# Group norm averages in 64x64 tiles, a split norm and a Strassen projection for the first image, two more output buffers

## The chip, the cores and the metric

The kernel runs on one core of a Trainium2 chip. The metric is the time of one execution on the device in microseconds (us). The core's engines are TensorE (PE; PEld is its weight load), VectorE (DVE), ScalarE (ACT), GpSimd (POOL) and SyncE (SP), which here only issues DMAs.

## What is computed

Input x has 8 images of 512 channels and 32x32 positions, all float32. The result is x plus the following, cut to what matters:

```
t  = silu(bn(conv1x1(group_norm(x))))           # 512 -> 512; halves y0, y1 of 256 channels
ys = [y0, y1]
for i in range(2):                               # two bottlenecks
    yi = ys[-1]
    z  = silu(bn(conv3x3(yi)))                   # 256 -> 256
    q, k, v = conv1x1(z), 3 x 256 channels       # 4 heads of 64
    z  = softmax(q (k + r)^T / 8) v              # over 1024 positions
    z  = silu(bn(conv1x1(z)))
    ys.append(yi + z)
out = x + silu(bn(conv1x1(concat(ys))))          # 1024 -> 512
```

The group norm has 32 groups of 16 channels: it needs the mean and the variance over 16 neighbouring partitions and all positions.

## The kernel before

An image lies in four tiles of 128 channels by 1024 positions (`xs`). The loop over the images works on one image at a time; the norm and first convolution (`cv1`) of the next image are worked into the first attention of the present one. Only the first image has its norm and `cv1` ahead of everything.

**The norm.** `gn_stats` takes mean and variance of each channel (L472, L473 on DVE). `gn_mean` averages over the 16 channels of a group by one matmul with the 128x128 matrix `gmat` (L478), four columns wide, and four small DVE steps form the deviations (L481 to L484). `gn_rstd` averages these by a second matmul (L489), DVE adds epsilon (L491), POOL takes the power -0.5 (L492), and DVE applies the norm in place, one 128x1024 pass for each tile (L506). `group_norm` is a generator that yields between these steps; for a later image each step is called from `behind`, between groups of attention.

**The opening.** SP loads four x tiles, the first raw 3x3 weights, then `w1` (1 MB, weights of `cv1`). DVE does the norm, then computes the 3x3 weights of the fast convolution (`make_u`, L316 to L331) and the batch norm scales `sh` and `bh`, and then the transformed image (`tiles_in`, L406 to L429). `cv1` is 32 matmuls of 128x512; float32 matmuls are two records each in the profile. Its lines show as L372, those of the 3x3 convolution as L921, with VectorE's `columns_out` and `rows_out` (L437 to L465) behind them; `z` then passes ScalarE's SiLU (L355).

**The projection.** `project` makes q, k and v by plain products (L372, L556). `project_strassen` makes them by Strassen's scheme, seven products in place of eight (L585, L589), from weight sums `sq` that `make_sq` computes and stores in DRAM and `load_sq` brings back. It is used for both bottlenecks from the second image on. It adds some DVE steps, in part behind the first logits (`add_r`, L606 and L607, and `later`).

**The attention.** `attention_fast` has four groups of eight steps in pairs: logits (L692), exponentials on ACT into `pt` (L696, three buffers), sums of these on DVE (L710, L712), products with v (L726) into the single buffer of `ps_av`. At a group's end, DVE evicts them (L734) and PE adds the sums up over partitions (`s_ps`, L744). Other work is called in the dictionary `behind`, by group, and by pair where a key has two numbers. In the first image's second attention these are

```python
behind = {1: ahead, NG: first, NG + 1: second}
if b == 0:
    behind |= {-1: load_ahead, 0: prepare, 2: lambda: make_sq(0), 3: lambda: make_sq(1)}
```

`prepare` is `make_ws`: four 128x1024 DVE steps (L172 to L175). `ahead` there runs `make_sw` (L249 to L252).

**The order.** A scheduler puts each engine's instructions in a fixed order, earlier written ones first where they are ready in its own estimate. `tc.issue_after(ins)` puts those instructions of its block that run on the engine of `ins` behind `ins`; it isn't a wait. Large weights share `ring`, five buffers of 1 MB; a load waits for a free one, and the loads behind it in SP's queue with it. PSUM has three buffers `ps_big` and one `ps_av`.

**The end.** `cv2` of the last image writes eight pieces of 128x512: an addition (L1180), SiLU, the addition of x (L1183), and a store from one of two buffers with tag `t`. Pieces of x come by POOL's queue into two buffers, each load behind the store of an earlier piece.

Of the kernel before, what the change touches and what calls it, by code (L numbers as in the profile page):

```python
# [44 lines left out]
F32 = mybir.dt.float32  # L45
# [16 lines left out]
def kernel(  # L62
# [41 lines left out]
        nc.sync.dma_start(xt, src)  # L104
        return xt

    xs = [load_x(act, 0, c, NX) for c in range(NX)]


    def ring(shape, name):  # L110
# [2 lines left out]
    def load_w1():  # L113
        w = ring([P, NX, 2 * C], "w1")
        nc.sync.dma_start(w, cv1_w.rearrange("(k p) o -> p k o", p=P))
        return w

    def load_w2(n=2):
        nk = (2 + N) * NM // 2
# [56 lines left out]
        last = [nc.gpsimd.dma_start(dst, w) for w, dst in zip(sums, s_dram2)][-1]  # L176
        return last, (a11, s1, a12, s4, s2, s3, a22)

    w1 = load_w1()

    NBN = 2 * NM + 2 * N * NM + NO
    bnp = const.tile([P, NBN, 4], F32, name="bnp")
# [33 lines left out]

    sq_dram = [tc.dram_tile([P, 4, 3, P], F32, name=f"sq{n}") for n in range(N)]

    def make_sq(n):
        (a11, a12), (a21, a22) = ([block_qkv(n, o, i) for i in range(2)] for o in range(2))  # L220
        parts = [act.tile([P, 2, 3, P], F32, tag="x", name="sq_new", bufs=NX) for _ in range(2)]
# [128 lines left out]
    def stages(act, small, ps_big, ps_av, n_pt):  # L350
# [3 lines left out]

            return nc.scalar.activation(dst, src, AF.Silu, scale=sh[:, k : k + 1], bias=bh[:, k : k + 1])  # L355

        silu_in = []

        def table_of(func):

# [2 lines left out]
        def conv1x1(w_of, rhs_of, nk, ks=None, ps=None, ends=None, by_half=False):  # L363


            if ps is None:
                ps = ps_big.tile([P, NH, HALF], F32, tag="big", name="ps")
            begin, end = ends or (0, nk - 1)
            ks = range(nk) if ks is None else ks
            order = [(k, half) for k in ks for half in range(NH)]  # L370
            for k, half in sorted(order, key=lambda a: a[1]) if by_half else order:
                nc.tensor.matmul(ps[:, half, :], w_of(k), rhs_of(k, half), start=(k == begin), stop=(k == end))  # L372
            return ps

        def tiles_in(yp):
# [96 lines left out]
                nc.vector.bn_stats(st[:, half, :], xt[:, ts(half, HALF)])  # L472
            nc.vector.bn_aggr(mv[:, c, :], st.rearrange("p a b -> p (a b)"))  # L473

        def gn_mean(mv):

            ps = ps_big.tile([P, NX], F32, tag="big", name="gm_ps")
            nc.tensor.matmul(ps, gmat, mv[:, :, 0], start=True, stop=True)  # L478
            gm = small.tile([P, NX], F32, tag="gm", name="gm")
            dev = small.tile([P, NX], F32, tag="dev", name="dev")  # L480
# [6 lines left out]
        def gn_rstd(dev):  # L487
            ps = ps_big.tile([P, NX], F32, tag="big", name="gv_ps")
            nc.tensor.matmul(ps, gmat, dev, start=True, stop=True)  # L489
            gr = small.tile([P, NX], F32, tag="gr", name="gr")  # L490
            nc.vector.tensor_scalar(gr, ps, GN_EPS, None, ALU.add)  # L491
            nc.gpsimd.tensor_tensor(gr, gr, mhalf[:, :NX], ALU.pow)  # L492
            return gr

        def group_norm(xts, between=None):


            mv = small.tile([P, NX, 2], F32, tag="mv", name="mv", bufs=2)

            def stats(cs):  # L500
                for c in cs:
                    gn_stats(mv, c, xts[c])

            def apply(cs, gm, gr):
                for c in cs:
                    last = nc.vector.tensor_scalar(  # L506
                        xts[c], xts[c], gm[:, c : c + 1], gr[:, c : c + 1], ALU.subtract, ALU.mult
                    )
# [8 lines left out]
            gr = gn_rstd(dev)  # L517
            if between is None:
                yield apply(range(NX), gm, gr)
                return  # L520
            with tc.issue_after(between().ins):
                last = apply(range(NX), gm, gr)
            yield last

        def project(n, z):

# [372 lines left out]
        def cv1(w, xts, y0, y1, ocs):  # L899

            for oc in ocs:
                ps = conv1x1(lambda k: w[:, k, ts(oc, P)], lambda k, half: xts[k][:, ts(half, HALF)], NX)
# [250 lines left out]
        def cv2(b, w2, ys, begun={}, parts={}):  # L1153

            def rows_of(dram, oc, half):
                if isinstance(b, int):
                    return dram[b, ts(oc, P), ts(half, HALF)]
                return dram[bass.ds(b, 1), ts(oc, P), ts(half, HALF)][0]  # L1160

            def residual(oc, half):
                t = act.tile([P, HALF], F32, tag="xr", name="x_res", bufs=2)
                nc.gpsimd.dma_start(t, rows_of(x, oc, half))
                return t

            pieces = [(oc, half) for oc in range(NO) for half in range(NH)]
            res = [residual(*pieces[0]), residual(*pieces[1])]
            for i, (oc, half) in enumerate(pieces):
                if half == 0:  # L1170
                    ks = range((2 + N) * NM)
                    if oc in begun:
                        ps = cv2_products(w2, ys, oc, ks[-NM:], begun[oc], by_half=oc == NO - 1)
                    else:
                        ks = ks[2 * NM if oc in parts else 0 :]
                        ps = cv2_products(w2, ys, oc, ks, ends=(ks[0], ks[-1]), by_half=oc == NO - 1)
                t = act.tile([P, HALF], F32, tag="t", name="t", bufs=2)
                src = ps[:, half, :]
# [47 lines left out]
    with tc.issue_after(made.ins):  # L1226
# [6 lines left out]
    with tc.issue_after(last.ins):  # L1233
# [6 lines left out]
    s.cv1(w1, xs, y0, ypad[0], [*Y1S, *Y0S])  # L1240
    with tc.issue_after(made.ins):
        vs = s.tiles_in(ypad[0])
    load_bottleneck(0)
# [1 line left out]
    for b in range(B):  # L1245
# [6 lines left out]
        def u_of(n):  # L1252
            def of(oc):
                nonlocal last_load
                if b == 0 and oc == 1:
                    if n == 0:
                        with tc.issue_after(last.ins):
                            for i in range(PAIRS):
                                make(n, oc, [i])
                    else:  # L1260
                        for k in range(NM):
                            raws[n, oc, k] = load_raw(n, oc, k, "kv"[k])
                        with tc.issue_after(last.ins):
# [240 lines left out]
```

## Time and profile before

| | before |
|---|---|
| median of 3 runs | 2328.49 us (2327.59 to 2328.65) |
| the profiled execution | 2328.05 us |
| its span, first to last instruction | 2326.2 us |
| mean granted TensorE clock | 0.998 |
| PE busy | 2293.7 us |
| DVE busy | 1827.8 us |
| first product of `cv1` | 15.93 us |
| first 3x3 product | 46.20 us |

A row of the timeline has the start in us, the duration, engine, line, operation, the tiles as out<-in with shapes, and the number of records merged in it; a bracket has the idle time of the engine before it and what ended that. A row of the waits has who waited for whom, the total in us, how many times, and the longest. In the page's group lines the last number after the bar is idle time.

### The profile page before, as it was taken

The page shows a single profiled execution, that of the slowest core. Times are in us where ns is not written, and L with a number is a line of the kernel's source. Part 1 is how long each engine was busy: PE and PEld are TensorE (multiplying, and loading weights), DVE is VectorE, ACT ScalarE, POOL GpSimd, SP SyncE. Part 2 cuts the span into 40 slices and gives each one's busy share as a digit, 9 for nine tenths or more (in the row PEclk, how much of TensorE's full clock was granted, in tenths as well). Part 3 has the DMA queues.
Part 4 walks back from the last instruction along what each step waited for, and adds up shares of the span by engine and source line. Part 5 has one row for each costly group of instructions (what it writes and reads, how often), then busy time and mean ns, then how long its engine had stood idle before and what let it go on. Part 6 is the DMA issues. An engine that isn't in the chain of part 4 may idle for free.

```text
span 2326.2 us, 36363 instructions
## 1 busy us (share of the span) xinstructions
PE 2293.7 (99%) x14746; PEld 1160.4 (50%) x14746; DVE 1827.8 (79%) x2899; ACT 980.6 (42%) x1282; POOL 88.9 (4%) x307
## 2 busy tenths in 40 slices
PE   7999999999999999999999999999999999999998
PEld 4536346363553636446364553635436364463633
DVE  8867877888788887888788887887877988777774
ACT  1442624536244352544525344253542535335352
POOL 1000100000000000000000000000000000000001
PEclk9999999999999999999999999999999999999999
DMA  7413334041430415213161221602116030250202
GB/s 256 155 54 109 111 102 189 16 150 33 143 143 15 150 34 190 101 39 122 52 225 48 73 88 51 249 29 98 62 47 249 29 133 29 80 205 16 87 11 70
DMA packets 95280, 234.80 MB, mean 101 GB/s; under 512 B 28032, under 2 KB 50496, under 8 KB 81664
## 3 DMA queue, kind: packets, MB, share of 16 engines
q1 hardware_dynamic: 83296, 182.05, 23.2%
q0 software_dynamic: 11808, 50.34, 5.7%
q8 instruction: 118, 1.93, 0.3%
q14 instruction: 58, 0.48, 0.1%
HBM read 197.75 MB, written 34.60 MB: 100 GB/s over the span
## 4 chain that ended last, share of the span: by engine, by line
PE 95%; DVE 3%; DMA 1%; ACT 0%; issue 0%; POOL 0%; SPq 0%; DVEq 0%; ACTq 0%
PE av_ps L726 19%; PE l_ps L692 19%; PE c_ps L921 14%; PE c L976 8%; PE p_ps L585 7%; PE x_ps L1088 6%; PE c_new L976 6%; PE m_ps L942 5%; PE ps L372 5%; PE pv_ps L589 3%; PE s_ps L744 1%; PE p_ps L589 1%; PE s_ps L762 1%; PE v_ps L556 1%; DVE acc L712 0%; DMA x_res<-in_x_dram 0%
## 5 line engine op out<-in xcount | busy, mean ns | idle before, releaser
L696 ACT ACTIVATE pt<-l_ps 128x1024 f32<-128x1024 f32 x512 | 494.9, 1023 | 408.4 <-PE l_ps L692 385.4
L712 DVE TENSOR_TENSOR acc<-acc,pt 128x1024 f32<-128x1024 f32 x384 | 469.5, 1223 | 65.4 <-ACT pt L696 40.3
L726 PE MATMUL av_ps<-pt,vT 64*64 64x512 f32 x4096 | 485.1, 591 | 1.1 <-DVE ao L734 1.1
L692 PE MATMUL l_ps<-q,kr 64*64 64x512 f32 x4096 | 484.1, 590 | 0.0
L921 PEld LDWEIGHTS c_ps<-v_in,u 128*128 128x128 f32 x2720 | 306.3, 192 | 7.9 <-issue 6.7
L921 PE MATMUL c_ps<-v_in,u 128*128 128x128 f32 x2720 | 306.9, 275 | 1.1 <-DVE v_in L429 1.1
L726 PEld LDWEIGHTS av_ps<-pt,vT 64*64 64x64 f32 x4096 | 152.0, 133 | 277.3 <-issue 230.7
L692 PEld LDWEIGHTS l_ps<-q,kr 64*64 64x64 f32 x4096 | 153.7, 133 | 269.7 <-issue 256.2
L436 ACT COPY m<-c_ps 128x256 f32<-128x256 f32 x96 | 35.5, 370 | 225.8 <-PE c_ps L921 220.8
L976 PE MATMUL c_new<-t_in,ws 128*128 128x512 f32 x288 | 124.6, 592 | 0.0
L942 PE MATMUL m_ps<-ao,m_sb 128*128 128x512 f32 x256 | 112.5, 592 | 0.0
L710 DVE TENSOR_TENSOR acc<-pt 128x1024 f32<-128x1024 f32 x64 | 78.1, 1220 | 27.3 <-ACT pt L696 27.3
L355 ACT ACTIVATE m_kept<-m_kept,bh,sh 128x512 f32<-128x512 f32 x42 | 31.9, 806 | 146.0 <-DVE m_kept L1060 86.3
L976 PEld LDWEIGHTS c_new<-t_in,ws 128*128 128x128 f32 x288 | 54.7, 190 | 68.9 <-issue 66.0
L355 ACT ACTIVATE t<-m_ps,bh,sh 128x512 f32<-128x512 f32 x64 | 48.0, 776 | 83.9 <-PE m_ps L942 82.5
L585 PE MATMUL p_ps<-t_z,sq 128*128 128x512 f32 x168 | 81.3, 593 | 0.0
L942 PEld LDWEIGHTS m_ps<-ao,m_sb 128*128 128x128 f32 x256 | 48.6, 190 | 61.2 <-issue 61.2
L950 DVE TENSOR_TENSOR ylast<-t,ypad 128x512 f32<-128x512 f32 x32 | 22.0, 692 | 63.2 <-ACT t L355 63.2
L355 ACT ACTIVATE z<-z,bh,sh 128x512 f32<-128x512 f32 x64 | 48.6, 806 | 50.9 <-DVE z L465 50.9
L429 DVE TENSOR_TENSOR v_in<-w_rows 128x512 f32<-128x512 f32 x96 | 65.9, 687 | 0.0
L976 PE MATMUL c<-ypad,ws 128*128 128x512 f32 x144 | 63.8, 592 | 0.0
L1088 PE MATMUL x_ps<-t_x,sw 128*128 128x512 f32 x144 | 62.8, 592 | 0.0
(252 smaller groups left out, 2952.1 us busy)
## 6 DMA issues: line engine op xcount, KB each, us to landing
u<-u SPq DMA_DIRECT2D x85, 1024.0 KB
x<-in_x_dram SPq DMA_DIRECT2D x32, 512.0 KB
x_res<-in_x_dram POOLq DMA_DIRECT2D x28, 512.0 KB, 6.8
out_dram<-m_kept POOLq DMA_DIRECT2D x28, 512.0 KB, 7.2
w<-in_cv_w_dram SPq DMA_DIRECT2D x13, 1024.0 KB
u<-u_new POOLq DMA_DIRECT2D x12, 1024.0 KB, 5.9
rs<-r_dram SPq DMA_DIRECT2D x96, 128.0 KB
ws<-s SPq DMA_DIRECT2D x24, 512.0 KB
```

Of the source, the lines that this page charges most:

```text
L355: return nc.scalar.activation(dst, src, AF.Silu, scale=sh[:, k : k + 1], bias=bh[:, k : k + 1])
L372: nc.tensor.matmul(ps[:, half, :], w_of(k), rhs_of(k, half), start=(k == begin), stop=(k == end))
L585: nc.tensor.matmul(ps[:, o, :], w[:, o, :], rhs, start=not onto, stop=True, skip_group_check=onto)
L589: nc.tensor.matmul(v[:, ts(j, P)], rhs[:, ts(j, P)], w[:, 2, :], start=j == 0 and not onto, stop=True, skip_group_check=True,)
L692: nc.tensor.matmul(ps[kh * HD : (kh + 1) * HD, hd, :], kr[r, c, o : o + HD], q[r, c, ts(half, HALF)], start=True, stop=True,)
L696: exp = nc.scalar.activation(pt[:, i], ps, AF.Exp, scale=SCALE)
L712: ins = nc.vector.tensor_tensor(accs[g], accs[g], pt[:, i], ALU.add)
L726: nc.tensor.matmul(avs[g][hd * HD : (hd + 1) * HD, kh, :], vT[r, j, o : o + HD], pt[r, i, hd, :], start=(j == 0), stop=(j == NJ - 1),)
L921: nc.tensor.matmul(ps[:, row, col, :], us[i][:, k, row, SLOT[col], :], vs[i][:, k, row, col, :], start=(k == 0), stop=(k == NM - 1),)
L942: nc.tensor.matmul(pss[oc][:, half, :], m2_sb[:, n, k, ts(oc, P)], ao[:, k, ts(half, HALF)], start=(k == 0), stop=(k == NM - 1),)
L976: nc.tensor.matmul(ps[:, o, :], w[:, k, ts(o, P)], rhs[part][:, c, :], start=(k == 0 and not onto), stop=(k == KB - 1), skip_group_check=onto,
L1088: nc.tensor.matmul(ps[:, o, :], w[:, c, ts(o, P)], rhs[c], start=(c == 0 and not onto), stop=(c == 1), skip_group_check=onto,)
```

## The change

The averages: each of the two matmuls of a norm becomes two matmuls with 64x64 blocks of `gmat`, one for each half of the partitions, for all images.

```diff
+        def over_groups(ps, src):
+            for h in range(2):
+                r = slice(h * HD, (h + 1) * HD)
+                ins = nc.tensor.matmul(ps[r], gmat[r, r], src[r], start=True, stop=True)
+            return ins
...
-        def gn_mean(mv):
-            ps = ps_big.tile([P, NX], F32, tag="big", name="gm_ps")
-            nc.tensor.matmul(ps, gmat, mv[:, :, 0], start=True, stop=True)
...
+        def gn_mean(mv, n=NX, pool=ps_big, tag="big"):
+            ps = pool.tile([P, n], F32, tag=tag, name="gm_ps")
+            over_groups(ps, mv[:, :, 0])
```

The first image's norm goes in two halves of two tiles. `w1` is loaded in halves, the first one ahead of x2 and x3. POOL computes a shift, and ScalarE applies the norm. Products of `cv1` with the first half of the channels are placed between the steps of the second half's norm.

```diff
-    xs = [load_x(act, 0, c, NX) for c in range(NX)]
+    xs = [load_x(act, 0, c, NX) for c in range(NX // 2)]
...
+    load_w1_half(0)
+    xs += [load_x(act, 0, c, NX) for c in range(NX // 2, NX)]
...
-    w1 = load_w1()
+    load_w1_half(1)
...
+        def group_norm_part(xts):
+            n = len(xts)
+            mv = small.tile([P, n, 2], F32, tag="mv", name="mv", bufs=2)
+            for c in range(n):
+                gn_stats(mv, c, xts[c])
+            yield
+            gm, dev = gn_mean(mv, n, ps_av, "av")
+            yield
+            gr, multiplied, read = gn_rstd(dev, n, ps_av, "av")
+            shift = small.tile([P, n], F32, tag="dev", name="shift")
+            nc.gpsimd.tensor_tensor(shift, gm, gr, ALU.mult)
+            nc.gpsimd.tensor_scalar(shift, shift, -1.0, None, ALU.mult)
+            for c in range(n):
+                applied = nc.scalar.activation(
+                    xts[c], xts[c], AF.Identity, scale=gr[:, c : c + 1], bias=shift[:, c : c + 1]
+                )
+            yield multiplied, read, applied
...
-    normed = [*s.group_norm(xs, lambda: make_u(2, u_first[2][:, 0], raws[0, 0, 0]))][-1]
+    Y_ORDER = [*Y1S, *Y0S]
+    _, _, (_, read, _) = s.group_norm_part(xs[: NX // 2])
+    norm = s.group_norm_part(xs[NX // 2 :])
+    with tc.issue_after(read.ins):
+        next(norm)
+    begun = {}
+    def begin(oc, ks):
+        begun[oc] = s.cv1_products(w1, xs, oc, ks, begun.get(oc))
+        return s.last_product[0]
+    first = begin(Y_ORDER[0], [0])
+    with tc.issue_after(first.ins):
+        next(norm)
+    begin(Y_ORDER[0], [1])
+    first = begin(Y_ORDER[1], [0])
+    with tc.issue_after(first.ins):
+        multiplied, normed, applied = next(norm)
+    with tc.issue_after(multiplied.ins):
+        begin(Y_ORDER[1], [1])
+        begin(Y_ORDER[2], range(NX // 2))
+    made = make_u(2, u_first[2][:, 0], raws[0, 0, 0])
     with tc.issue_after(normed.ins):
         made = make_u(0, u_first[0][:, 0], raws[0, 0, 0])
```

`last_product` is the last matmul that `conv1x1` issued. `cv1` gets `begun` and goes on from the third channel tile where a product is begun. The last two steps of the first 3x3 weights are also put behind `applied`.

The first image's second bottleneck projects by Strassen. Its `make_sq(1)` moves from the third group of that attention to the end of the first attention, into another buffer.

```diff
-                if b > 0 and oc == 1:
+                if (b > 0 or n > 0) and oc == 1:
                     sq[n], last_load = load_sq(n)
...
         def second():
+            if b == 0:
+                make_sq(1, "xr", 2)
...
-            behind |= {-1: load_ahead, 0: prepare, 2: lambda: make_sq(0), 3: lambda: make_sq(1)}
+            behind |= {-1: load_ahead, 0: prepare, 2: lambda: make_sq(0, "x", NX)}
```

The last two of the eight output pieces take their tile from tag `h`, which also has two buffers:

```diff
-                t = act.tile([P, HALF], F32, tag="t", name="t", bufs=2)
+                t = act.tile([P, HALF], F32, tag="t" if i + 2 < len(pieces) else "h", name="t", bufs=2)
```

More of the change, by code (lines that the diff above doesn't have):

```diff
@@ L116, in load_w1, with load_w1_half @@
         return w
+    w1 = ring([P, NX, 2 * C], "w1")
+    def load_w1_half(i):
+        ks = slice(i * NX // 2, (i + 1) * NX // 2)
+        nc.sync.dma_start(w1[:, ks], cv1_w.rearrange("(k p) o -> p k o", p=P)[:, ks])
+    load_w1_half(0)
+    xs += [load_x(act, 0, c, NX) for c in range(NX // 2, NX)]
     def load_w2(n=2):
@@ L217, with make_sq @@
     sq_dram = [tc.dram_tile([P, 4, 3, P], F32, name=f"sq{n}") for n in range(N)]
-    def make_sq(n):
+    def make_sq(n, tag, bufs):
         (a11, a12), (a21, a22) = ([block_qkv(n, o, i) for i in range(2)] for o in range(2))
-        parts = [act.tile([P, 2, 3, P], F32, tag="x", name="sq_new", bufs=NX) for _ in range(2)]
+        parts = [act.tile([P, 2, 3, P], F32, tag=tag, name="sq_new", bufs=bufs) for _ in range(2)]
         s1, s2, s3, s4 = (t[:, j] for t in parts for j in range(2))
@@ L355, in silu @@
             return nc.scalar.activation(dst, src, AF.Silu, scale=sh[:, k : k + 1], bias=bh[:, k : k + 1])
-        silu_in = []
+        silu_in, last_product = [], [None]
         def table_of(func):
@@ L371, in conv1x1 @@
             for k, half in sorted(order, key=lambda a: a[1]) if by_half else order:
-                nc.tensor.matmul(ps[:, half, :], w_of(k), rhs_of(k, half), start=(k == begin), stop=(k == end))
+                last_product[0] = nc.tensor.matmul(
+                    ps[:, half, :], w_of(k), rhs_of(k, half), start=(k == begin), stop=(k == end)
+                )
             return ps
@@ L473, in gn_stats @@
             nc.vector.bn_aggr(mv[:, c, :], st.rearrange("p a b -> p (a b)"))
-        def gn_mean(mv):
-            ps = ps_big.tile([P, NX], F32, tag="big", name="gm_ps")
-            nc.tensor.matmul(ps, gmat, mv[:, :, 0], start=True, stop=True)
-            gm = small.tile([P, NX], F32, tag="gm", name="gm")
-            dev = small.tile([P, NX], F32, tag="dev", name="dev")
+        def over_groups(ps, src):
[6 more added lines that the diff above has]
+            over_groups(ps, mv[:, :, 0])
+            gm = small.tile([P, n], F32, tag="gm", name="gm")
+            dev = small.tile([P, n], F32, tag="dev", name="dev")
             nc.vector.tensor_copy(gm, ps)
@@ L485, in gn_mean, with gn_rstd, group_norm @@
             return gm, dev
[L487 to L495, printed above, removed]
+        def gn_rstd(dev, n=NX, pool=ps_big, tag="big"):
+            ps = pool.tile([P, n], F32, tag=tag, name="gv_ps")
+            ins = over_groups(ps, dev)
+            gr = small.tile([P, n], F32, tag="gr", name="gr")
+            read = nc.vector.tensor_scalar(gr, ps, GN_EPS, None, ALU.add)
+            nc.gpsimd.tensor_tensor(gr, gr, mhalf[:, :n], ALU.pow)
+            return gr, ins, read
+        def group_norm_part(xts):
[13 more added lines that the diff above has]
+                    xts[c], xts[c], AF.Identity, scale=gr[:, c : c + 1], bias=shift[:, c : c + 1]
+                )
+            yield multiplied, read, applied
+        def group_norm(xts):
             mv = small.tile([P, NX, 2], F32, tag="mv", name="mv", bufs=2)
@@ L516, in group_norm @@
             yield
[L517 to L523, printed above, removed]
+            yield apply(range(NX), gm, gn_rstd(dev)[0])
         def project(n, z):
@@ L897, in attention_general, with cv1_products, cv1 @@
             return ao
-        def cv1(w, xts, y0, y1, ocs):
+        def cv1_products(w, xts, oc, ks=range(NX), ps=None):
+            return conv1x1(
+                lambda k: w[:, k, ts(oc, P)], lambda k, half: xts[k][:, ts(half, HALF)], NX, ks, ps, (0, NX - 1)
+            )
+        def cv1(w, xts, y0, y1, ocs, begun={}):
             for oc in ocs:
-                ps = conv1x1(lambda k: w[:, k, ts(oc, P)], lambda k, half: xts[k][:, ts(half, HALF)], NX)
+                ks = range(NX // 2 if oc in begun else 0, NX)
+                ps = cv1_products(w, xts, oc, ks, begun.get(oc))
                 for half in range(NH):
@@ L1232 @@
             last = nc.vector.tensor_scalar(sh[:, at : at + NM], sh[:, at : at + NM], -1 / 12, None, ALU.mult)
-    with tc.issue_after(last.ins):
+    with tc.issue_after(last.ins), tc.issue_after(applied.ins):
         for i in (1, 2):
@@ L1239 @@
     y0 = new_y0()
-    s.cv1(w1, xs, y0, ypad[0], [*Y1S, *Y0S])
+    s.cv1(w1, xs, y0, ypad[0], Y_ORDER, begun)
     with tc.issue_after(made.ins):
```

## The prediction

> **What bounds the kernel now.** I read the page first: busy time by engine, then the chain that ended last.
>
> ```profile
> PE 2293.7 (99%) x14746; PEld 1160.4 (50%) x14746; DVE 1827.8 (79%) x2899; ACT 980.6 (42%) x1282; POOL 88.9 (4%) x307
> PE 95%; DVE 3%; DMA 1%; ACT 0%; issue 0%; POOL 0%; SPq 0%; DVEq 0%; ACTq 0%
> ```
>
> TensorE is the bound: 32.5 us of the 2326.2 us span are not PE. PE work that goes is worth its full time, unless another engine then ends the same stage. So I went to the stages that the edits touch, first the waits of PE:
>
> ```profile
> PE gm_ps L478 <- DVE mv L473: 11.0, 1, 11.0
> PE ps L372 <- DVE x L506: 2.2, 1, 2.2
> PE ps L372 <- ACT z L355: 2.1, 2, 1.2
> PE c_ps L921 <- DVE u_new L326: 1.3, 1, 1.3
> PE c_ps L921 <- DVE u_new L330: 1.2, 1, 1.2
> ```
>
> All lie in the first image. PE's first product starts at 15.93 us, but at 62 to 65 us PE waits for VectorE's u tiles, and at 76.01 for z. The timeline of VectorE between says why:
>
> ```profile
> 15.07 2.98 DVE L506 TENSOR_SCALAR x<-x,gm,gr 128x1024 f32<-128x1024 f32 x4 [1.16 <-POOL gr L492]
> 17.96 0.55 DVE L321 TENSOR_TENSOR u_new<-raw 128x384 f32<-128x384 f32 x1
> ...
> 74.69 0.42 DVE L465 SCALAR_TENSOR_TENSOR z<-sd,r_ends 128x256 f32<-128x256 f32 x1
> ```
>
> From L321 to L465 VectorE waits only 0.9 us (L406 for the second SiLU) and 0.2 us (L437). **The opening is VectorE's up to 76 us**: what counts there is when L321 starts, not when PE starts.
>
> For the averages of the later norms, the timeline of PE around one:
>
> ```profile
> 140.43 1.95 PE L726 MATMUL av_ps<-pt,vT 64*64 64x512 f32 x16
> 142.31 0.39 PE L489 MATMUL gv_ps<-dev,gmat 128*128 128x4 f32 x2
> 142.63 1.95 PE L692 MATMUL l_ps<-q,kr 64*64 64x512 f32 x16
> ```
>
> Sixteen such matmuls take 1.72 us start to start elsewhere (129.45 to 131.17). Here it is 2.20, of which 0.05 belong to the sums before; the next batch loses 0.05. So a 0.25 us matmul pair costs PE 0.48 us.
>
> **What the Trainium skill says.** "TensorEngine Tiling (Array Packing)", Key Properties: changing the tiling mode drains TensorE. The trace agrees: the 0.48 us. The same page, Gotcha 1, says that different row tiles can't access one PSUM bank at the same time; the new pair writes two halves of one bank, and no run here shows that. "TensorE: Matmul & The Clock Gate", Part 1: an idle array runs at half rate until some 3.4 us of activity. In the trace cv1's first six records are 0.85 us apart, up to 21.2 us, then 0.43: 5.3 us of half rate. "ScalarE: Activation LUTs", Table sets: identity is in every set, so I charge no table load for the new Identity passes; no run here shows it yet.
>
> **The opening.** x0 and x1 go first; half of w1 (512 KB) comes before x2 and x3. Loads of 512 KB landed some 1.5 us apart, so x3 is ready near 10.9 instead of 9.4. Statistics of x0 and x1: done at 7.1 (4.30 + 2 x 1.4). First average: 0.74 us to the copy, as now (10.83 to 11.57), four small DVE steps 0.85, second average 0.7: read at 9.6. POOL: 0.1 + 0.7 for two columns (1.04 for four, 3.15 for sixteen) + two new small steps 0.5. Then ScalarE, about 1.0 us for a 128x1024 pass as in its Exp rows (1.02): x0 at 12.0. **PE starts at 12.0, 3.9 us earlier.** w1's half is there.
>
> The other half: statistics follow the first read on DVE (9.6 to 12.4, x3 landing included). Its first average stands on PE behind two products, four records at 0.85: 15.4. DVE has its variance at 16.9. The second average stands behind eight more records, some still at half rate: 20.3; **the read on DVE is at 20.9**. Everything that VectorE does next is put behind this read, where today it starts at 17.96. Moving four applications (2.98 us) to ScalarE doesn't make up for it, since DVE idles meanwhile, but for L317 to L319. So DVE is 3.0 us later; it then meets no wait for the SiLUs (1.1 us gone), and some of the 2.1 us of second-bottleneck u work between 66.9 and 74.5 may fall behind z. I take **+1.5 us at 76 us**. Ends: read at 14.7 if PE held nothing up, -2 with fills left; read at 22.5 with both averages behind all twelve records, +3.5. PE's own lead ends as a longer wait for u. SP issues one DMA more; raw lands about 1.5 us later, while DVE is idle. POOL's new steps end before its 16-column power is wanted.
>
> **Averages in 64x64 tiles.** Seven later norms, two averages each: 14 x 0.48 = 6.7 us now. In the new form nothing drains; left are four short matmuls and two exposed 64-column loads (133 ns each against 187 for 128, partly overlapped): I estimate 0.19 us. Gain 14 x 0.29 = **-4.1 us**. Ends: 0 if one bank serialises them as a drain does, -6.7 if they are free.
>
> **First image's second projection by Strassen.** Now, and for a Strassen projection with the start of the attention:
>
> ```profile
> 208.59 3.60 PE L372 MATMUL ps<-z,qkv_sb 128*128 128x512 f32 x8
> 231.63 0.66 PE L692 MATMUL l_ps<-q,kr 64*64 64x512 f32 x4
> 250.22 1.95 PE L726 MATMUL av_ps<-pt,vT 64*64 64x512 f32 x16 [0.63 <-DVE ao L734]
> 367.30 1.88 PE L585 MATMUL p_ps<-z,qkv_sb 128*128 128x512 f32 x4
> 391.21 1.22 DVE L710 TENSOR_TENSOR acc<-pt 128x1024 f32<-128x1024 f32 x1
> 397.41 5.21 DVE L712 TENSOR_TENSOR acc<-acc,pt 128x1024 f32<-128x1024 f32 x4
> 402.54 0.68 DVE L734 TENSOR_TENSOR ao<-av_ps,ao 128x512 f32<-128x512 f32 x1
> ```
>
> The plain one takes 208.59 to 231.63, 23.0 us. Strassen takes 367.30 to 385.75, 18.45 us; here z comes 2 us later (L465 is 5.2 us after the convolution, there 3.2), and t1 queues on DVE: some 1.1 + 0.8 us of wait. So 20.3: **-2.7 us**.
>
> Then VectorE. With Strassen its first sum starts 5.46 us after the first logits (385.75 to 391.21), here 3.13 (231.63 to 234.76); add_r of the second half adds 2.4. In the image with Strassen shown, the eviction L734 begins 16.8 us after the logits and is just in time. But the first image's group 0 also holds make_ws, L172 to L175, 238.56 to 243.23: 4.67 us that run right behind the second pair's sums. Behind them queue the later sums and L734; PE's s_ps and next av wait for those, ps_av being a single buffer. L734 would end at 17.47 + 4.67 = 22.1 us, PE's av begin at 22.2 after the logits, against 18.59 now: **+3.6 us**. In group 1 DVE needs 14.0 us of PE's 14.5, so the stall isn't repeated. Net **+0.9 us**. Ends: -3.3 if make_ws falls into a gap, +2.5 with one more us for evictions of p_ps on ScalarE.
>
> make_sq(1) moves into the end of the first attention: four DVE ops, 2.2 us, fit the 2.32 us before 155.01 where DVE waits for a DMA, and its two POOL writes go where POOL idles. load_sq takes one ring buffer, so the second w2 load starts at about 205 instead of 198, over 30 us before its use; SP has nothing urgent behind it. Zero.
>
> **The end.** The last piece's t now waits at 2318.12 for an earlier store (1.62 us). With its own buffer, that goes; next comes x_res, for which L1183 waits at 2320.03, behind unchanged POOL stores. So **-0.2** for a less crowded last store; ends 0 and -0.7.
>
> Sum: 1.5 - 4.1 + 0.9 - 0.2 = -1.9 us. Against the profiled execution: span 2326.2 to 2324.3 (its own time 2328.05, 1.85 outside the span). Its time is 0.4 under the median 2328.49, which becomes **2326.6**. About 0.2%, 4.7 us, is what a measurement of this kernel tells from no change.
>
> **Rivals.** *Covered*: make_ws or its queue doesn't hold L734 up (-3.6) and the opening's DVE delay is taken out by the u work that moves (-1.5): 2321.5. For it: no wait of PE lies after 330 us. Against: VectorE's unbroken rows. *The change doesn't do what it says*: the 64x64 pair costs as much as the 128x128 one, no -4.1: 2330.7. For it: the shared bank. Against: attention's own 64x64 matmuls flow at 0.43 us per four. *Slower*: the second half's averages hold VectorE. Place: the read of the second average; price: 1 us for each us. From 22.8 us the whole is slower than before; at 24.3, with PE at half rate through all twelve records, it is 2330.0, and slower by 0.2% from 27.5. For it: PE's in-order queue and its half rate. Against: 5.3 us of half rate would be over at 17.3.
>
> **How the numbers follow.** Forecast 0.49, covered 0.32, same-cost tiles 0.07, held read 0.12. Faster by over 0.2%: covered and 0.02 of the forecast's edge, 0.34. Slower by over 0.2%: 0.07, the far half of the held read. Same: 0.59. The range 2320 to 2331 reaches past covered and same-cost, leaving about 0.15 out.
>
> **What would show it.** PE's first product near 12; the second-half read near 20.9 and z's L465 near 76; records around each average 1.9 us apart, not 2.2; first logits of the second attention about 20.3 us after its convolution; L734 with some 4 us of PE wait there; last L1183 still on x_res. If L734 isn't waited for, or PE waits for u less than now, I am wrong towards faster.

## The result and the profile after

| | before | after |
|---|---|---|
| median of 4 runs each, side by side | 2328.04 us (2327.21 to 2328.65) | 2328.56 us (2327.69 to 2329.48) |
| ratio | | 1.0003, 95% interval 0.9985 to 1.0020 |
| the profiled execution, its span | 2328.05, 2326.2 us | 2328.13, 2326.7 us |
| mean granted TensorE clock | 0.998 | 0.995 |

No change that can be measured. The forecast was 2326.6 us with "no change" as the likeliest case. But the zero is made of terms of up to 6 us, and only some of them have the predicted size. The page first: busy time by engine, and the chain that ended last. Line numbers are those of the kernel that a row comes from. In the changed kernel L617 and L621 are products of the projection by Strassen, L724 the logits, L758 the products with v (`av_ps`), L744 the sums, L766 the eviction and L776 `s_ps`.

```profile
PE 2292.5 (99%) x14806; PEld 1175.1 (51%) x14806; DVE 1837.1 (79%) x2918; ACT 986.2 (42%) x1287; POOL 90.9 (4%) x312
PE 93%; DVE 4%; DMA 1%; ACT 0%; issue 0%; SPq 0%; POOL 0%; DVEq 0%; ACTq 0%
```

PE is busy for 1.2 us less, though an eighth of a projection's products and the draining averages are gone: something made other PE work longer. And DVE has 4% of the chain where it had 3%. The waits of PE say where (who waited for whom; us in total, times, longest):

```profile
...
PE c_ps L959 <- DVE u_new L331: 4.7, 1, 4.7
PE s_ps L776 <- DVE acc L744: 4.3, 1, 4.3
PE ps L381 <- ACT x L529: 2.9, 1, 2.9
PE p_ps L617 <- issue: 2.0, 1, 2.0
...
PE av_ps L758 <- DVE ao L766: 0.5, 1, 0.5
```

The u wait is where PE's lead of the opening ended, as foreseen, 4.7 us for 2.5 before. The s_ps wait is the group 0 stall. "issue" at L617 hides t1: its step on DVE (L644) runs from 212.90 to 213.58, and PE goes on at 213.67. To place all this I compared when stages start in the two traces:

| up to | before | after | difference | what this stage adds |
|---|---|---|---|---|
| first 3x3 product | 46.20 | 42.31 | -3.89 | |
| first logits, first attention | 92.56 | 93.59 | +1.03 | opening +1.03 |
| second bottleneck's first 3x3 product | 187.02 | 187.34 | +0.32 | one norm's averages -0.71 |
| first logits, second attention | 231.63 | 231.18 | -0.45 | projection -0.77 |
| second image's first 3x3 product | 345.87 | 351.76 | +5.89 | attention +6.34 |
| last 1x1 product behind attention | 2287.94 | 2289.52 | +1.58 | six norms -4.31 |
| end of the span | 2326.19 | 2326.65 | +0.46 | end -1.1 |

**Opening.** VectorE's timeline: the second half's read, the u work behind it, and the last step of z.

```profile
20.01 0.16 DVE L510 TENSOR_SCALAR gr<-gv_ps 128x2 f32<-128x2 f32 x1 [3.10 <-PE gv_ps L491]
20.08 0.55 DVE L330 TENSOR_TENSOR u_new<-raw 128x384 f32<-128x384 f32 x1
...
75.73 0.41 DVE L476 SCALAR_TENSOR_TENSOR z<-sd,r_ends 128x256 f32<-128x256 f32 x1
```

The read is at 20.01 (forecast 20.9), u starts at 20.08 where it started at 17.96, and the last step of z starts 1.04 us later than before (74.69). In each of the thirteen profiles of this document the first logits follow this step by 17.86 or 17.87 us: when VectorE is done with z decides the opening.

**Averages.** PE's timeline around one of them:

```profile
141.11 1.95 PE L758 MATMUL av_ps<-pt,vT 64*64 64x512 f32 x16
142.87 0.17 PE L491 MATMUL gv_ps<-dev,gmat 64*64 64x4 f32 x1
142.88 0.65 PE L724 MATMUL l_ps<-q,kr 64*64 64x512 f32 x2
142.89 0.23 PE L491 MATMUL gv_ps<-dev,gmat 64*64 64x4 f32 x3
142.96 1.93 PE L724 MATMUL l_ps<-q,kr 64*64 64x512 f32 x14
144.65 1.94 PE L758 MATMUL av_ps<-pt,vT 64*64 64x512 f32 x15
```

The small matmuls run in among the logits. From 141.11 to 144.65 there are 3.54 us for two batches of 1.72: the average costs PE 0.1 us, where it cost 0.48. The two halves of one PSUM bank, a risk in the prediction, serialise nothing that can be seen.

**Projection and attention.** PE's timeline, from the first product on z to the sums of group 0:

```profile
208.90 1.88 PE L617 MATMUL p_ps<-z,qkv_sb 128*128 128x512 f32 x4
...
213.67 3.38 PE L617 MATMUL p_ps<-t_z,sq 128*128 128x512 f32 x4 [2.00 <-issue]
...
231.18 3.66 PE L724 MATMUL l_ps<-q,kr 64*64 64x512 f32 x32
...
252.89 1.08 PE L776 MATMUL s_ps<-acc,ones 128*32 128x256 f32 x8 [4.31 <-DVE acc L744]
253.91 3.69 PE L758 MATMUL av_ps<-pt,vT 64*64 64x512 f32 x16
```

Look at the durations of equal work. Four p_ps records take 1.88 us at 208.90, and 3.38 behind the wait of 2.00; sixteen av_ps records take 1.90 us elsewhere, and 3.69 behind the wait of 4.31. The busy time by stretch has, behind the bounds and the length, the busy time and count of PE, PEld, DVE, ACT and POOL, and then the granted clock, the DMA share and GB/s:

```profile
58.10:62.00 3.90, 3.59 (x15) 3.33 (x16) 3.90 (x10) 2.09 (x4) 0.41 (x1) 0.50 0.00 0
214.10:217.50 3.40, 3.40 (x8) 1.66 (x7) 1.78 (x5) 2.48 (x3) 0.00 (x0) 0.51 0.00 0
251.60:255.00 3.40, 2.11 (x16) 0.72 (x20) 3.30 (x4) 0.90 (x2) 0.00 (x0) 0.50 0.47 193
255.00:258.40 3.40, 3.40 (x24) 0.96 (x20) 3.29 (x5) 0.00 (x0) 0.00 (x0) 0.50 0.03 2
```

**Behind each of the three longer waits in the middle of the kernel, TensorE ran at half rate for 3.4 or 6.8 us.** The profile of before has that only at the start and the end. This is what the prediction had left out.

**Group 0's stall.** VectorE's timeline in it:

```profile
243.20 1.22 DVE L181 TENSOR_TENSOR s<-w,w 128x1024 f32<-128x1024 f32 x1
...
246.60 1.22 DVE L744 TENSOR_TENSOR acc<-acc,pt 128x1024 f32<-128x1024 f32 x1
247.74 1.22 DVE L184 TENSOR_TENSOR s<-w,s 128x1024 f32<-128x1024 f32 x1
248.87 3.87 DVE L744 TENSOR_TENSOR acc<-acc,pt 128x1024 f32<-128x1024 f32 x3
252.66 0.69 DVE L766 TENSOR_TENSOR ao<-av_ps,ao 128x512 f32<-128x512 f32 x1
```

The four steps of `make_ws` (L181 to L184) stand ahead of the last sums, and these ahead of s_ps and the eviction L766, with no gap between them: the mechanism of the prediction, row by row.

**The end**, VectorE's last two rows of the pieces:

```profile
2318.91 0.69 DVE L1221 TENSOR_TENSOR t<-t,x_res 128x512 f32<-128x512 f32 x1 [0.23 <-ACT t L364]
2320.89 0.69 DVE L1221 TENSOR_TENSOR t<-t,x_res 128x512 f32<-128x512 f32 x1 [1.29 <-DMA x_res<-in_x_dram]
```

The wait for an earlier store is gone, and the last addition waits for x_res instead, as predicted.

### The profile page after: what moved, and what is told of

It is laid out like the page before. It is cut to its first block, busy times and chain, and to the rows that moved or that the text cites. A ratio compares the mean times of both kernels' runs of the same rounds, so it can differ in the third digit from the quotient of the medians.

```text
span 2326.7 us, 36527 instructions
## 1 busy us (share of the span) xinstructions
PE 2292.5 (99%) x14806; PEld 1175.1 (51%) x14806; DVE 1837.1 (79%) x2918; ACT 986.2 (42%) x1287; POOL 90.9 (4%) x312
## 3 DMA queue, kind: packets, MB, share of 16 engines
q8 instruction: 119, 1.95, 0.3%
## 4 chain that ended last, share of the span: by engine, by line
PE 93%; DVE 4%; DMA 1%; ACT 0%; issue 0%; SPq 0%; POOL 0%; DVEq 0%; ACTq 0%
PE av_ps L758 19%; PE l_ps L724 18%; PE c_ps L959 14%; PE c L1014 8%; PE p_ps L617 8%; PE x_ps L1126 6%; PE c_new L1014 6%; PE m_ps L980 5%; PE ps L381 3%; PE pv_ps L621 3%; PE s_ps L776 1%; PE p_ps L621 1%; PE s_ps L794 1%; DVE acc L744 1%; DMA w<-in_cv_w_dram 0%
## 5 line engine op out<-in xcount | busy, mean ns | idle before, releaser
L744 DVE TENSOR_TENSOR acc<-acc,pt 128x1024 f32<-128x1024 f32 x384 | 469.4, 1222 | 68.7 <-ACT pt L728 43.0
L758 PE MATMUL av_ps<-pt,vT 64*64 64x512 f32 x4096 | 488.2, 593 | 0.5 <-DVE ao L766 0.5
L724 PE MATMUL l_ps<-q,kr 64*64 64x512 f32 x4096 | 486.5, 591 | 0.0
L758 PEld LDWEIGHTS av_ps<-pt,vT 64*64 64x64 f32 x4096 | 159.4, 133 | 270.5 <-issue 226.1
L724 PEld LDWEIGHTS l_ps<-q,kr 64*64 64x64 f32 x4096 | 160.2, 133 | 264.4 <-issue 253.2
L742 DVE TENSOR_TENSOR acc<-pt 128x1024 f32<-128x1024 f32 x64 | 78.1, 1220 | 20.9 <-ACT pt L728 20.9
L617 PE MATMUL p_ps<-t_z,sq 128*128 128x512 f32 x180 | 88.5, 602 | 2.0 <-issue 2.0
L448 DVE TENSOR_TENSOR r_mid<-c_ps,m 128x256 f32<-128x256 f32 x64 | 27.0, 422 | 45.6 <-ACT m L447 45.6
```

The source lines that it names most:

```text
L617: nc.tensor.matmul(ps[:, o, :], w[:, o, :], rhs, start=not onto, stop=True, skip_group_check=onto)
L724: nc.tensor.matmul(ps[kh * HD : (kh + 1) * HD, hd, :], kr[r, c, o : o + HD], q[r, c, ts(half, HALF)], start=True, stop=True,)
L742: return nc.vector.tensor_tensor(accs[g], pt[:, 0], pt[:, 1], ALU.add)
L744: ins = nc.vector.tensor_tensor(accs[g], accs[g], pt[:, i], ALU.add)
L758: nc.tensor.matmul(avs[g][hd * HD : (hd + 1) * HD, kh, :], vT[r, j, o : o + HD], pt[r, i, hd, :], start=(j == 0), stop=(j == NJ - 1),)
```

## The experiments

My theory: the change's parts add up as in the table, and what the Strassen part loses beyond the prediction is the half rate behind waits. Its rivals: the wait lengths alone did it (no clock), the stall isn't `make_ws`, and the opening is bound by something other than VectorE. In the ratios that follow, each kernel is set against the kernel before, run on the same chip (2327.66, 2327.62 and 2327.33 us in the three sets).

### The averages alone

The kernel before, with only the averages changed:

```diff
-            nc.tensor.matmul(ps, gmat, mv[:, :, 0], start=True, stop=True)
+            over_groups(ps, mv[:, :, 0])
...
-            nc.tensor.matmul(ps, gmat, dev, start=True, stop=True)
+            over_groups(ps, dev)
```

> The kernel before with one edit: the averages of every norm in two 64x64 matmuls. If a mode change's drain was the cost: each later image's first attention is 0.71 to 0.72 us shorter, seven times, so 5.0 us in all, nothing else moves, median 2323.1 against 2328.0. The prediction's estimate was 4.1. If the gain seen in the changed kernel belongs to something else in it: nothing.

Measured: 2322.09 us, ratio 0.9976 (0.9967 to 0.9986). Each of the seven later norms takes 0.71 to 0.72 us out, 5.0 together, and nothing else moves in the middle of the kernel. Confirmed. In this profile the opening was 0.39 us later, with only its two averages edited, and the end 1.25 shorter, with nothing edited: those two stages vary by themselves.

### Without the Strassen projection

The changed kernel with the first image's plain projection:

```diff
-                if (b > 0 or n > 0) and oc == 1:
+                if b > 0 and oc == 1:
...
-            if b == 0:
-                make_sq(1, "xr", 2)
...
-            behind |= {-1: load_ahead, 0: prepare, 2: lambda: make_sq(0, "x", NX)}
+            behind |= {-1: load_ahead, 0: prepare, 2: lambda: make_sq(0, "x", NX), 3: lambda: make_sq(1, "x", NX)}
```

> The changed kernel with the first image's second bottleneck projected plainly again (its weight sums made in the third group as before). Theory, VectorE queue and clock: the two half-rate stretches at 214 and 252 us and the 4.3 us wait of s_ps go; from that bottleneck's 3x3 start to its m2 start 117.6 us as before instead of 123.2, so 5.6 us less, median 2322.9. Rival, that Strassen's saved product pays and the rest is lost elsewhere: 2 to 3 us more than the changed kernel, 2331.

Measured: 2322.90 us, ratio 0.9978 (0.9970 to 0.9987). From the second bottleneck's 3x3 product to the second image nothing is lost (both come 0.19 us later than before), where the whole change loses 5.6. **Strassen costs this version 5.6 us, not 0.9.** The half rate at 214 and 252 is gone with it; that at 57 stays.

### The old opening

The changed kernel, with the order of loads, the whole norm on VectorE and the u transforms of before:

```diff
-    xs = [load_x(act, 0, c, NX) for c in range(NX // 2)]
+    xs = [load_x(act, 0, c, NX) for c in range(NX)]
...
-    load_w1_half(1)
+    w1 = load_w1()
...
+    normed = [*s.group_norm(xs, lambda: make_u(2, u_first[2][:, 0], raws[0, 0, 0]))][-1]
```

> The changed kernel with the opening of before (one norm for all four tiles on VectorE, w1 in one load, no product of cv1 ahead). Theory, VectorE bounds the opening: first logits at 92.6 instead of 93.6, the wait of PE for u short again and no half-rate stretch at 57 us; 1.0 us less, median 2327.5. Rival, PE's earlier start pays: 2 to 4 us more than the changed kernel.

Measured: 2327.08 us, ratio 0.9996 (0.9987 to 1.0004). First logits at 93.47: only 0.1 us sooner than with the new opening, so my number was missed. In the opening its trace has a half-rate stretch that before's hasn't, from 64.8 to 68.2, behind two waits for u of 1.3 and 1.2 us that before has as well. And behind t1 the clock stayed up this time, with a wait as long as the changed kernel's. Its row of PE:

```profile
213.57 1.95 PE L619 MATMUL p_ps<-t_z,sq 128*128 128x512 f32 x4 [2.00 <-issue]
```

The same wait of 2.00 us, then 1.95 us for what took 3.38. So a wait of this length doesn't always cost the clock. The projection came to -2.43 here, near the predicted -2.7.

### PE kept busy in the two waits

The changed kernel with idle PE time filled. The added matmuls go into PSUM that the following product overwrites; their results are never read. `fill` is 4 in the first image's second bottleneck.

```diff
+            for _ in range(fill):
+                nc.tensor.matmul(ps_b[:, 0, 0:256], gmat, z[:, 0, 0:256], start=True, stop=True)
             product(ps_b, ps_v[:, 1], s1, t1)
...
+                for _ in range(9 if sq is not None and at == NM * NH and g == 0 else 0):
+                    nc.tensor.matmul(ps, gmat, q[:, 0, 0:NQ4], start=True, stop=True)
```

> The changed kernel with matmuls that nobody reads put into PE's two waits of the first image's second bottleneck: four of 128x256 ahead of the second Strassen product (1.7 us), nine ahead of the first s_ps (3.8 us). Theory, clock: the waits stay as long, but no half rate follows at 214 and 252 us: 1.7 and 2.8 us less, 4.5 in all, median 2324.1. Rival, the time is the waits' own length alone: no change, or slower by what the fill overruns.

Measured: 2324.56 us, ratio 0.9986 (0.9979 to 0.9993). The busy time by stretch of this kernel:

```profile
214.10:217.50 3.40, 3.40 (x14) 2.09 (x15) 1.78 (x4) 2.06 (x3) 0.00 (x0) 1.00 0.00 0
251.60:255.00 3.40, 3.40 (x36) 1.20 (x40) 3.19 (x4) 0.38 (x2) 0.00 (x0) 1.00 0.12 45
```

And its timeline of PE, at the batch that took 3.69 us in the changed kernel:

```profile
252.12 1.95 PE L761 MATMUL av_ps<-pt,vT 64*64 64x512 f32 x16
```

The clock is 1.00 in both places, and the same av_ps batch is back at 1.95 us. Projection -2.46 (changed kernel -0.77), attention +3.63 (+6.34): 4.4 us gained by adding work, without shortening either wait (s_ps still starts 21.6 us behind the first logits, 21.7 in the changed kernel). **This separates the two parts of the loss: the wait, and the clock behind it.** Without the clock's part both terms are close to those of the prediction (-2.7 and +3.6), and av starts 22.2 us behind the first logits (252.12 less 229.90), the very number that was forecast.

### make_ws two groups later

```diff
+        def strassen_ready():
+            nonlocal three
+            prepare()
+            three = s.strassen(b, ws, y0, y1)
+            for i in range(PAIRS):
+                us[0, i] = load_u(0, 0, i)
...
-            behind |= {-1: load_ahead, 0: prepare, 2: lambda: make_sq(0, "x", NX)}
+            behind |= {-1: load_ahead, 2: strassen_ready, 3: lambda: make_sq(0, "x", NX)}
```

> The changed kernel, but make_ws of the first image (with the Strassen part that needs its sums) issued behind group 2 of the second attention, where it was behind group 0, and make_sq(0) behind group 3 instead of 2. If the long wait of PE in group 0 is make_ws standing between VectorE's sums and the eviction (my step of the prediction), the 4.3 us wait at the first sum matmul goes, and with it the half-rate stretch at 251.6: the stretch from first logits to the second image shrinks from 79.4 by about 6.3 us, to the 73.0 of the kernel before. Span 2320.5, time 2322. Part of it may come back in group 2: VectorE has about 0.5 us of slack a group there, so up to 2 us of wait. Rival: the wait comes from the Strassen projection's own evictions on VectorE, which begin the sums 2.3 us later; then at most 1 to 2 us go. Rival: DMA of the stores made by make_ws collides with the next image's loads in its new place; then waits of PE after 330 us appear.

Measured: 2323.78 us, ratio 0.9985 (0.9978 to 0.9992); span of the profile 2321.3. From the first logits of the second attention to the 1x1 product behind it 74.05 us pass, where the changed kernel has 79.4: 5.3 of the 6.3 us are gone, and s_ps isn't waited for. One wait of PE is new:

```profile
PE c L1014 <- DVE ao L766: 1.6, 1, 1.6
```

It is the backlog that was expected to come back in part. SyncE's rows, store and reload of the softmax reciprocals, show where VectorE lost time ahead of it:

```profile
273.73 0.32 SPq L822 DMA_DIRECT2D r_dram<-rc  x1
281.08 2.00 SPq L824 DMA_DIRECT2D rs<-r_dram  x2
```

They stand 7.4 us apart (1.6 and 1.4 in this kernel's groups before and behind), and VectorE waited 5.0 us for that. The long wait in group 0 was `make_ws`. What delays the reload is open. At that time POOL's queue had two stores of 1 MB by `make_ws`, issued at 270.16 and 271.42 and landed by 278.05, and behind them two loads of x_res, the last of which landed at 280.84. In the changed kernel a pair stands 4.5 us apart as well (262.76 and 267.23), but 13 us behind the stores of `make_ws`, which had landed by 253.78, and beside the loads of x_res. No run separates the two.

### t1 not held back

```diff
-            with tc.issue_after(mid.ins):
+            if first_image:
                 tt(t1, b12, b11, ALU.subtract)
+            else:
+                with tc.issue_after(mid.ins):
+                    tt(t1, b12, b11, ALU.subtract)
```

> The changed kernel, but in the first image t1, the first difference of the Strassen projection, isn't held behind the middle row's combination: VectorE can take it in the 2.7 us that it idles before 208.9. Then PE's second product starts right behind the first (211.7 instead of 213.67): no wait of 2.0 us and no half-rate stretch (1.7 us). A shorter wait, about 1.1 us, is left at the third product, for z of the second half. First logits of the second attention 2.8 us earlier (1.1 us counted), so second projection -3.6 against before where the changed kernel has -0.8; the wait in group 0 of 4.3 us and its half rate stay. Time 2325.7. If the half-rate stretch isn't a consequence of the wait it stays, and only 1.0 us is gained.

Measured: 2325.05 us, ratio 0.9991 (0.9984 to 0.9998). PE's timeline:

```profile
212.03 1.88 PE L617 MATMUL p_ps<-t_z,sq 128*128 128x512 f32 x4
...
216.21 1.98 PE L617 MATMUL p_ps<-z,qkv_sb 128*128 128x512 f32 x4 [1.41 <-ACT z L364]
```

No wait ahead of the second product, 1.4 us ahead of the third (1.1 expected), no half rate in the projection; behind the wait in group 0 a stretch of 3.4 us stays. The projection is -3.0 against before: short of -3.6 by 0.3 us of wait and by a part that I can't place.

### The u transform in VectorE's gaps

```diff
-    with tc.issue_after(normed.ins):
+    with tc.issue_after(made.ins):
         made = make_u(0, u_first[0][:, 0], raws[0, 0, 0])
```

> The changed kernel, but the u transform that waited for the second half's read on VectorE (make_u(0) of the first image) now follows the transform before it, so VectorE can work in the 2.1 and 3.1 us that it idles at 14.1 and 16.9. My theory: the opening is VectorE's up to 76 us, so about 4 of these 5.2 us come back: first logits at 89.6 instead of 93.6, the 4.7 us wait of PE for u near 57 falls under 1 us and the half-rate stretch 57.0 to 63.9 goes. Time 2324.5. Rival: VectorE then waits for the SiLUs or for the second raw tile, and it all comes back there: first logits within 0.5 us of 93.6. Rival: the reads of the averages are pushed back by the new instructions ahead of them (0.55 us each) and PE's first convolution with them: 1 us lost.

Measured: 2325.04 us, ratio 0.9988 (0.9980 to 0.9997). First logits at 90.92, 2.7 us sooner, where 4 were expected. Of the 5.2 us of idle time 1.7 are left. PE's wait for u is 1.6 us and two shorter ones, but together they still put the clock down from 61.4 to 64.8; VectorE then waits 1.4 us for c_ps. So VectorE does bound the opening, and the clock took part of the gain. The rivals fall: the reads are at 16.18 and 20.49, 0.0 and 0.5 us later.

### The end alone

```diff
-                t = act.tile([P, HALF], F32, tag="t", name="t", bufs=2)
+                t = act.tile([P, HALF], F32, tag="t" if i + 2 < len(pieces) else "h", name="t", bufs=2)
```

> The kernel before with only the end changed: the last two pieces of the output use buffers of their own. From the prediction: 0.2 us less. From the stage sums of the changed kernel: 1.1 us less. But the kernel with the averages alone had the same 1.2 us less behind its last 1x1 product (37.0 instead of 38.25) with the end as before, so I now expect that the 1.1 us aren't the buffers': the 1.6 us wait for an earlier store goes, the last addition still waits for x_res, and the time is within 1 us of the kernel before, 2327.5 to 2328.

Measured: 2327.72 us, ratio 0.9999 (0.9990 to 1.0008): no effect that can be measured. The profile of this run gave something else. Its opening is before's, instruction for instruction, yet first logits come at 93.98 instead of 92.56. The busy time of this stretch, first in this run:

```profile
65.00:68.50 3.50, 3.50 (x20) 3.50 (x19) 3.41 (x10) 0.00 (x0) 1.06 (x2) 0.51 0.59 220
```

And in the profile of before:

```profile
65.00:68.50 3.50, 3.50 (x33) 3.50 (x33) 3.50 (x11) 0.29 (x1) 1.06 (x2) 1.00 0.57 218
```

20 matmul records where there were 33. **Even the opening of the kernel before pays for a half-rate stretch in some executions, and not in others.** That is 1.4 us of spread, and it explains the miss with the old opening: from the first 3x3 product to the first logits 47.98 us pass in that run and in this one, and 46.36 us in the two profiles without the stretch (before, and the averages alone).

### All repairs together

The three edits (u in the gaps, t1 early, `make_ws` later) on the changed kernel; the second version also moves make_sq(0) behind the last group.

> The changed kernel with the three repairs together: the u transform in VectorE's gaps, t1 early, make_ws behind group 2 and make_sq(0) behind group 3. If they add: 2.7 us (opening) + 2.2 (projection) + 5.4 (attention) off the changed kernel's span of 2326.7, so 2316.4, time 2318. No half rate at 214 and none in the second attention; in the opening one 3.4 us stretch near 61 stays (waits of 2.2 us in one window). A wait of PE of about 1.6 us for ao stays at the end of the last group. Rival: the earlier opening shifts DMA against the second attention, and make_ws in its new place costs more than 1.6 us there: 2320.

> As the run before, but make_sq(0) of 2.2 us leaves group 3 and is issued one step after the last group. If the 1.6 us wait of PE for ao at the end of the last group is VectorE's backlog, of which these 2.2 us are a part, the wait goes: span 1.5 us less, 2315, time 2316.7. Rival: the backlog comes from the 5.0 us wait for the softmax reciprocals' reload (their store and reload stood 7.4 us apart while make_ws's 2 MB went out), so the wait only shrinks or is moved: within 0.5 us of the run before.

Measured: 2316.65 us, ratio 0.9956 (0.9942 to 0.9971), and 2316.54 us, ratio 0.9954 (0.9940 to 0.9968). Both are some 11 us faster than the kernel before and 12 us faster than the changed kernel (2328.88 us in the same set). Spans 2313.9 and 2314.7, where the parts' sum was 2316.4: the repairs add, and a little more than expected. In the first the half-rate stretch that I expected in the opening didn't come (2.0 us), and the wait at the end of the last group was 0.9 us, not 1.6. This wait is gone in the second, whose second attention is 0.9 us shorter, where I had expected 1.5. In the medians that doesn't show, because the openings, equal in code, differ by 2.0 us at the first logits (88.89 and 90.89). The busy time by stretch, of the first version:

```profile
59.50:63.00 3.50, 2.56 (x18) 2.21 (x19) 3.50 (x12) 0.00 (x0) 0.53 (x1) 1.00 0.29 88
```

And of the second:

```profile
61.40:64.80 3.40, 3.08 (x14) 3.08 (x15) 3.40 (x11) 0.00 (x0) 1.07 (x2) 0.50 0.38 155
```

The same small waits for u, full clock in one and half in the other. Of the 2.0 us, 0.64 are there at the first 3x3 product already; the rest comes in behind it, where the clock differs.

### The changed kernel again

> The changed kernel once more, nothing edited, to see how its half-rate stretches fall. In ten profiles so far every change of the granted clock lies a whole number of 3.413 us windows behind the first rise (12.0, 14.0, 58.0, 59.0, 69.0, 71.0 in the changed kernel's). If an idle window decides, not the wait: all changes again on that grid; the 4.7 us wait for u always drops the clock (a whole window is idle), the 4.3 us wait too; the 2.0 us wait at 211.7 only if it lies within one window, in which 2.0 us idle. Time 2328, and first logits at 93.6 within 0.5. Rival: a wait over some length drops the clock by itself: changes off the grid, and always the same stretches.

Measured: 2328.88 us, ratio 1.0005 (0.9997 to 1.0014). The clock changes at 12, 14, 58, 59, 69 and 71 windows of 3.413 us behind its first rise: on the grid, and in the same places. First logits at 94.78, outside the half us that I allowed: this stage varies more than I thought.

## Why the prediction was right

The sum was -1.9 us and the profiled spans gave +0.5; both lie within what can be told from no change. Step by step:

| step | predicted | measured | |
|---|---|---|---|
| opening | +1.5 | +1.03 in the profile, some +0.6 over all | right in kind; sign likely, size open |
| averages | -4.1 | -5.0 | right, undersized |
| Strassen projection | -2.7 | -0.77; -2.46 with the clock kept up | mis-sized |
| stall in group 0 | +3.6 | +6.34; +3.63 with the clock kept up | mis-sized |
| `make_sq(1)`, load_sq | 0 | no wait of PE belongs to them | right |
| end | -0.2 | -1.1 in the profile, none in the run of its own | open |

- **The Strassen terms failed in size, and by one cause.** "1.1 + 0.8 us of wait" was 2.0, and "PE's av begin at 22.2 after the logits" was right for the wait. So the rival in which `make_ws` doesn't hold the eviction up falls. What the sum lacked was the clock: 1.7 us behind the first wait and 2.7 behind the second. These are about half of PE's busy time in the stretches (3.4 us, and 6.8 less 1.3 of idle time). The prediction had quoted the rule on an idle array, and used it only for the opening's first records.
- **The averages** were estimated at 0.19 us each; they cost about 0.12 (0.36 saved of 0.48). The rival of same-cost tiles falls.
- **The opening** is VectorE's, as said: PE's 3.9 us came to nothing, and filling VectorE's gaps gave 2.7 to 4.7 us. The half rate reaches VectorE there too: in the changed kernel it waits 0.7 us for a product at 69.5 (0.2 in before's opening), 0.1 in the repaired run at full clock and 1.4 in the one at half rate. Over all profiles first logits are at 92.56, 92.95, 93.47 and 93.98 with the old opening, and from 93.46 to 94.78 with the new one (six profiles, the three with VectorE's gaps filled apart). The medians are 0.6 us apart, less than the spread of either: the sign is likely, the size open. The rival of the held read falls: the read came at 20.0, not at 22.8 or later. A slip in the sums didn't matter: the terms for the first half's read make 9.4 us, not 9.6, and it came at 9.15.
- **The end**: in before's profile, 38.25 us lie between the last 1x1 product and the end; in the other twelve 37.0 to 37.7, and 37.0 with the averages alone, which has the old buffers. So before's profile had an unlucky end, and the buffers needn't have given anything. When x_res lands decides, and that wasn't varied.

So it was right for the wrong proportions: averages and end 1.8 us better than forecast, opening 0.5 better, Strassen 4.7 worse. That these came to only 2.4 us in sum is luck.

## What to carry to other kernels

Price a wait of the bounding TensorE twice: its length, and the half-rate stretch that may follow. Here a wait of 2 us mostly cost 1.7 more, and one of 4.3 cost 2.7 more, so removing such a wait is worth more than its length, and filling it with useless matmuls gets the second part back (4.4 us for the two). When a part brings work to a second engine, list what already queues there in the same group: `make_ws` did little harm in group 0 (0.6 us of wait) until the sums began 2.3 us later, and two groups on it cost some 1 us.

## What the hardware showed beyond expectation

- Every change of the granted clock inside the kernel, in 13 profiles, lies a whole number of 3.413 us windows behind the first rise to full rate. The Trainium skill, "TensorE: Matmul & The Clock Gate", section "What's actually happening", gives such a free-running window of 3413 ns, and says that it makes the transition vary; the traces agree. Its table has the clock drop after at least one idle window, and there the runs say more: 2.0 us of idle time in a window of 3.413 was enough at 211.7.
- Where the limit lies: summing PE's idle time in each window, none with up to 1.63 us dropped the clock, and all with 2.2 us or more did. In between it went both ways (1.69, 1.96, 1.99 and 2.00 dropped it; 1.80, and 1.98 twice, did not), so it isn't idle time by the records alone. What else counts is open.
- The clock came back behind the first window in which PE idled for under 0.4 us. A wait that goes on in the window behind the one that dropped the clock so costs two windows of half rate, as at 57 and 252 (1.4 and 1.3 us of idle time in the second window).
- Two of ScalarE's Identity passes over 128x1024 took 2.37 us, where the prediction had charged about 1.0 us each. No table load came with them, as it had assumed: the profiles before and after both have 33 table loads in all, none of them next to these passes.
